# A graph network on one core: the weights' product in four pieces, deviations of x for up to four row tiles at once, a projection's two copies side by side

## The chip, the cores and the metric

The kernel runs on one core of a Trainium2 chip. The metric is the device time of one execution in microseconds (us); the time before is the median of three runs. One more execution was recorded by the hardware profiler; the page, the timelines and the waits below are of that one.

## The reference, cut to what matters

Two layers work on x (3327 rows of 256) and a sparse matrix adj (3327 x 3327). The change lies ahead of the first attention of layer 0; what it touches is the normalised input h, the keys and queries, and the products of h with U1.

```
h = maximum(layernorm(x), 0)            # rows: (x - mean) / sqrt(var + 1e-5)
# layer 0, two steps n; Xf = Xa = h at first
R = (adj + I) / rowsum
q = Xa @ W1.T @ W2.T ;  k = Xa @ W3.T
A = top_p(softmax(q @ k.T), 0.9)        # keep the largest until 0.9, rescale
Xf = R @ Xf ;  Xa = A @ Xa
Z += Xf @ U1[n].T + Xa @ U2[n].T
x = x + layernorm(h + Z)
# layer 1: h = maximum(layernorm(x), 0), attention over neighbours, elu
x = x + elu(attend(h @ W, adj))
```

## The kernel before, in words

Rows are padded to 26 tiles of 128. The work is cut into pieces, each a Python function with an engine, a length in us, a rank and needs. Class Plan (L470) plays these pieces through with the lengths it was given and lists them in the order in which they would start; L564 then issues them in that order. On the chip each engine runs its own list strictly in order and waits on semaphores, so a length is no time on the chip: it only settles the order. "take" and "give" count buffers (two px banks of PSUM, two pl, three kq, four mv, and so on), so that a piece that can't have its buffer is put later.

The start of the kernel goes like this. Function weights (L689) is one piece on PE: it issues the DMAs of W1, W2, W3, U1, U2 on ACT's queue, turns W1 (L703), copies it (L705), multiplies it by W2 (L707) and copies the product into wqk (L709), once for each half of 128 input columns. SP issues the 26 loads of x (L1725). Function prepare (L1108) then makes nine kinds of piece for each row tile t:

- DVE: mean and variance of the tile (measure, L673: L676, L678);
- POOL: 1/sqrt(var + eps) and -mean times that (L681: L683, L684, L686), on one column each;
- ACT: h = relu(x * scale + bias), in place (L1118);
- PE: two transposes of h into a pl bank (L1123); DVE copies them to c (L1126);
- PE: projection by wqk into a px bank (L1131), which gives keys on one half of the partitions and queries on the other;
- ACT: copy to kq (L1137), and of the queries' half straight into qq (L1138);
- POOL: the keys' half from kq to kt (L1141); SP: a DMA of the queries' half to the other half of the partitions of qq (L1144). kq is given back when both are done;
- for even t, sums of keys and their products: a transpose (L745), an ACT copy (L749), a product (L754) and additions to gk on DVE (L766).

Function project_u (L1163) multiplies c of a tile by both steps' U1 into one px bank (L1169), ACT copies one half of the result to main (L1172) and DVE the other half back to c (L1173), after ACT. These 26 products are wanted by the full products (class Full, L1052, with L1074) and can lie anywhere after prepare of their tile.

After the keys of all tiles come statistics of the logits (stats, L770: L781, L786, L792 and on, with a power on POOL at L811), and for each row tile a search (L1368): logits (L856), exponentials on ACT (L870), the row's sum (L879), a guess (POOL L883 to L885, ACT L890 to L893), counts of 3327 columns on ACT (L907) with steps on POOL (L916 on), a window on DVE (L962, L967), and the dropping of what is too small (L1017). Then attention (L1420) turns the row's weights (L1030), ACT copies them (L1035) and PE multiplies (L1042).

```
L1727        weighed = plan.put("PE", 3.0, -200.0, weights, lag=2.0)
L1728        loads = [plan.put("SP", 0.58, -200.0 + t, load_x, t) for t in range(NT)]
L1729        parts = [prepare(t, loads[t]) for t in range(NT)]
L1732        sources = [project_u(t, -1.9 + 0.001 * t) for t in range(NT)]
```

Of the kernel before, what the change touches and what calls it, by code (L numbers as in the profile page):

```python
# [10 lines left out]
F32 = mybir.dt.float32  # L11
# [4 lines left out]
ALU = mybir.AluOpType  # L16
# [3 lines left out]
P = 128  # L20
N = 3327
NT = 26
NP = NT * P
D = 256
DA = 64
# [5 lines left out]
LN_EPS = 1e-5  # L31
# [15 lines left out]
PIECES = 16  # L47
# [5 lines left out]
BUFS = dict(kk=2, e=4, sc=6, f=3, xa=2, xt=2, kq=3, ystage=2, base=1, mv=4, cum=2)  # L53
# [517 lines left out]
def fast(  # L571
# [18 lines left out]
    V, S, T, GP = nc.vector, nc.scalar, nc.tensor, nc.gpsimd  # L590
# [3 lines left out]
    ident = const.tile([P, P], F32, name="ident")  # L594
# [19 lines left out]
    powers = const.tile([P, 4], F32, name="powers")  # L614
# [10 lines left out]
    def half_of(t):  # L625

        r = side(t)
        lo = t // 8 * 512 + (t % 4 * P if t < NT - 1 else 0)
        return slice(r * DA, r * DA + DA), slice((1 - r) * DA, (2 - r) * DA), slice(lo, lo + P)

    with ExitStack() as l0:
        wpool = l0.enter_context(tc.tile_pool(name="wpool", bufs=1))
        small = l0.enter_context(tc.tile_pool(name="small", bufs=2))
# [15 lines left out]
        qq = wpool.tile([P, NT, P], F32, name="qq")  # L649
# [9 lines left out]
        wqk = wpool.tile([P, 2, 2, P], F32, name="wqk")  # L659
# [13 lines left out]
        def measure(src):  # L673

            st = small.tile([P, V.BN_STATS_DIM], F32, name="bst", bufs=3)
            V.bn_stats(st, src)  # L676
            mv = small.tile([P, 4], F32, name="mv", bufs=4)
            V.bn_aggr(mv[:, :2], st)  # L678
            return mv

        def reciprocal_deviation(mv, both=True):  # L681

            GP.tensor_scalar(mv[:, 2:3], mv[:, 1:2], LN_EPS, None, ALU.add)  # L683
            GP.tensor_tensor(mv[:, 2:3], mv[:, 2:3], powers[:, 0:1], ALU.pow)  # L684
            if both:
                GP.tensor_scalar(mv[:, 3:4], mv[:, 0:1], -1.0, mv[:, 2:3], ALU.mult, ALU.mult)  # L686


        def weights():  # L689
            w1 = etpool.tile([P, 4, P], F32, name="et")  # L690
            w1 = w1[:, 0, :].rearrange("p (c o) -> p c o", c=2)
            w2 = small.tile([P, PIECES, 8], F32, name="cands").rearrange("p c r -> p (c r)")[:DA, :DA]
            nc.scalar.dma_start(w1, w1t.rearrange("(c p) o -> p c o", p=P))
# [132 lines left out]
        plan = Plan(dict(rows=1, pl=2, px=2, acca=1, accf=1, accf0=1, accf1=1, et=3, at=4, y=1, e2=3, mask=2, **BUFS))  # L826

        class Row:

# [195 lines left out]
            def turn(self, g):  # L1025
                m = min(4, NT - 4 * g)
                pt = self.pt[g] = ps_x.tile([P, 4, P], F32, name="px")
                for k in range(m):
                    j = 4 * g + k
                    T.transpose(pt[:, k, :], self.e[:, j * P : (j + 1) * P], ident)  # L1030
# [21 lines left out]
        class Full:  # L1052
# [55 lines left out]
        def prepare(t, load):  # L1108
            mine, other, cols = half_of(t)
            held = {}  # L1110
            h = rhs[0][:, t, :]

            def first():
                held["mv"] = measure(h)

            def relu():
                mv = held["mv"]
                S.activation(h, h, AF.Relu, bias=mv[:, 3:4], scale=mv[:, 2:3])  # L1118

            def turn():  # L1120
                held["pt"] = ps_l.tile([P, 2, 512], F32, name="pl")
                for k in range(2):
                    T.transpose(held["pt"][:, 0, k * P : (k + 1) * P], h[:, k * P : (k + 1) * P], ident)  # L1123

            def copy():
                V.tensor_copy(c[:, t, :], held["pt"][:, 0, :D])  # L1126

            def project():
                ps = held["ps"] = ps_x.tile([P, P], F32, name="px")
                for k in range(2):  # L1130
                    T.matmul(  # L1131
                        ps, wqk[:, k, side(t), :], c[:, t, k * P : (k + 1) * P], start=(k == 0), stop=(k == 1)
                    )

            def share():
                held["kq"] = small.tile([P, P], F32, name="kq", bufs=BUFS["kq"])
                S.copy(held["kq"], held["ps"])  # L1137
                S.copy(qq[other, t, :], held["ps"][other])  # L1138

            def keys():  # L1140
                GP.tensor_copy(kt[mine, cols], held["kq"][mine])  # L1141
# [5 lines left out]
            a = plan.put("DVE", 0.62, r, first, needs=[load], take=["mv"])  # L1147
            a = plan.put("POOL", 1.1, r, lambda: reciprocal_deviation(held["mv"]), needs=[a])
            a = hs[0][t] = plan.put("ACT", 0.6, r, relu, needs=[a], give=["mv"])
# [12 lines left out]

        def project_u(t, rank):  # L1163
            held = {}

            def product():
                ps = held["ps"] = ps_x.tile([P, 2 * D], F32, name="px")
                for k in range(2):
                    T.matmul(ps, c[:, t, k * P : (k + 1) * P], u1[:, k, :], start=(k == 0), stop=(k == 1))  # L1169
# [3 lines left out]
            e = plan.put("DVE", 0.43, -2.6, lambda: V.tensor_copy(c[:, t, :], held["ps"][:, D:]), needs=[b], give=["px"])  # L1173
            return b, e

        def finish1(row, done, rank):
# [550 lines left out]
        weighed = plan.put("PE", 3.0, -200.0, weights, lag=2.0)  # L1727
        loads = [plan.put("SP", 0.58, -200.0 + t, load_x, t) for t in range(NT)]  # L1728
        parts = [prepare(t, loads[t]) for t in range(NT)]  # L1729
        keys, sums = [a for a, _ in parts], [b for _, b in parts]  # L1730
        layer1_ready = None
        sources = [project_u(t, -1.9 + 0.001 * t) for t in range(NT)]  # L1732
        right, fresh, failed = None, None, []
        for n in range(STEPS):
# [7 lines left out]
            for k in range(3):  # L1742
                p = stats(cuts[k], cuts[k + 1], base + (-50.0, -2.35, 0.0)[k], [keys, fresh], scaled)
# [102 lines left out]
```

## Time and profile before

| what | value |
|---|---|
| median of 3 runs | 2241.94 us (2241.08 to 2243.65) |
| the profiled execution's own time | 2240.52 us |
| its span, first to last instruction | 2238.6 us |
| PE, DVE, ACT, POOL busy, share of the span | 97%, 72%, 65%, 41% |
| granted TensorE clock, mean | 0.994 |
| PE busy from 0 to 10 us / from 10 to 15 us | 0.88 / 3.71 us |
| key copies of tiles to kt (L1141) | 26, from 15.30 to 55.10 us |
| first statistics product (L781) / first logits (L856) | 58.30 / 59.06 us |
| first transposes of row 0 (L1030) | 111.55 us |

How to read the profile: a group's line gives the source line, the engine, the operation, output <- inputs, shapes and count, then its busy time, the mean length of one in ns, and the idle time of the engine ahead of it with what ended that. A timeline line gives start and length in us, and in brackets how long the engine had been idle and on what. A line of the stage view gives the stretch, its length and each engine's busy time with its number of instructions. A PE product of two operands shows as two records, a transpose as one. ACT's first operation, a table load at 7.91 us, stands behind the DMAs that ACT issues itself.

### The profile page before, as it was taken

The page shows a single profiled execution, that of the slowest core. Times are in us where ns is not written, and L with a number is a line of the kernel's source. Part 1 is how long each engine was busy: PE and PEld are TensorE (multiplying, and loading weights), DVE is VectorE, ACT ScalarE, POOL GpSimd, SP SyncE. Part 2 cuts the span into 40 slices and gives each one's busy share as a digit, 9 for nine tenths or more (in the row PEclk, how much of TensorE's full clock was granted, in tenths as well). Part 3 has the DMA queues.
Part 4 walks back from the last instruction along what each step waited for, and adds up shares of the span by engine and source line. Part 5 has one row for each costly group of instructions (what it writes and reads, how often), then busy time and mean ns, then how long its engine had stood idle before and what let it go on. Part 6 is the DMA issues. An engine that isn't in the chain of part 4 may idle for free.

```text
span 2238.6 us, 36037 instructions
## 1 busy us (share of the span) xinstructions
PE 2177.3 (97%) x11978; PEld 1537.8 (69%) x11978; DVE 1615.0 (72%) x4229; ACT 1455.7 (65%) x2795; POOL 925.1 (41%) x2214
## 2 busy tenths in 40 slices
PE   7999999999999999999999999999999999999997
PEld 5487778777887778877878887887887433333332
DVE  5576657546655744178979877888777998989895
ACT  5776686566566652478887877878774455464653
POOL 6455355435544541256656666566653200000000
PEclk9999999999999999999999999999999999999998
DMA  3012221212212222621212222222225344444341
GB/s 99 20 38 70 68 70 54 70 49 64 70 53 70 70 83 67 191 76 56 76 49 70 59 74 72 81 62 66 69 75 154 121 129 137 116 144 119 102 128 42
DMA packets 192036, 183.76 MB, mean 82 GB/s; under 512 B 15354, under 2 KB 146144, under 8 KB 191712
## 3 DMA queue, kind: packets, MB, share of 16 engines
q1 hardware_dynamic: 189856, 180.10, 27.6%
q8 instruction: 96, 1.57, 0.3%
q10 hardware_dynamic: 1984, 1.26, 0.2%
q14 instruction: 100, 0.82, 0.1%
HBM read 164.41 MB, written 15.94 MB: 81 GB/s over the span
## 4 chain that ended last, share of the span: by engine, by line
PE 75%; ACT 8%; POOL 6%; DVE 5%; issue 3%; DMA 1%; SPq 0%; ACTq 0%; POOLq 0%; DVEq 0%
PE acca L1042 20%; PE accf L1074 20%; PE pl L1608 12%; PE px L1030 6%; PE pl L856 6%; ACT junk L907 5%; PE acca L1622 3%; PE accf L1622 3%; PE px L1217 2%; POOL sc L920 1%; PE px L1312 1%; PE px L1169 1%; DVE cands L967 1%; DVE y L962 1%; ACT et L1035 1%
## 5 line engine op out<-in xcount | busy, mean ns | idle before, releaser
L1042 PE MATMUL acca<-rhs,et 128*128 128x256 f32 x2704 | 619.4, 380 | 1.0 <-ACT et L1035 0.9
L907 ACT ACTIVATE junk<-e,sc 128x3327 fp8e5<-128x3327 f32 x182 | 559.2, 3073 | 48.1 <-POOL sc L952 46.8
L1042 PEld LDWEIGHTS acca<-rhs,et 128*128 128x128 f32 x2704 | 499.9, 191 | 64.4 <-ACT et L1035 2.9
L1074 PE MATMUL accf<-c,at 128*128 128x256 f32 x1352 | 313.5, 382 | 5.5 <-ACT f L1081 5.5
L1074 PE MATMUL accf<-main,at 128*128 128x257 f32 x1352 | 312.0, 382 | 5.6 <-DMA at<-in_adjt_dram 5.3
L962 DVE SCALAR_TENSOR_TENSOR y<-e,sc 128x1664 f32<-128x1664 f32 x104 | 209.0, 2010 | 149.0 <-POOL sc L949 147.0
L1074 PEld LDWEIGHTS accf<-main,at 128*128 128x128 f32 x1352 | 252.8, 191 | 47.9 <-issue 6.5
L1074 PEld LDWEIGHTS accf<-c,at 128*128 128x128 f32 x1352 | 250.0, 190 | 47.7 <-ACT f L1081 10.3
L1035 ACT COPY et<-px 128x512 f32<-128x512 f32 (+1 forms) x364 | 192.7, 553 | 136.1 <-PE acca L1042 72.9
L967 DVE MAX8 cands<-y 128x8 f32<-128x208 f32 x832 | 242.6, 361 | 3.6
L1017 DVE SCALAR_TENSOR_TENSOR e<-e,thr 128x832 f32<-128x832 f32 x208 | 213.1, 1082 | 2.2 <-DVE thr L1012 0.5
L870 ACT ACTIVATE e<-pl 128x1024 f32<-128x1024 f32 x208 | 179.0, 864 | 37.7 <-PE pl L856 37.5
L1581 ACT ACTIVATE et<-at 128x448 bf16<-128x448 f32 (+1 forms) x204 | 112.2, 550 | 137.3 <-DVE e L1592 81.5
L1030 PE MATMUL px<-ident,e 128*128 128x128 f32 x1352 | 191.2, 275 | 9.2 <-DVE gk L766 4.5
L1030 PEld LDWEIGHTS px<-ident,e 128*128 128x128 f32 x1352 | 159.5, 141 | 51.8 <-issue 15.3
L1608 PE MATMUL pl<-e,main 128*64 128x416 f32 x1024 | 187.2, 515 | 0.0
L856 PE MATMUL pl<-kt,qq 64*128 64x512 f32 (+1 forms) x832 | 173.5, 535 | 0.0
L1608 PEld LDWEIGHTS pl<-e,main 128*64 128x64 f32 x1024 | 71.0, 137 | 107.3 <-issue 92.0
L1592 DVE SCALAR_TENSOR_TENSOR e<-c,low,et 128x832 f32<-128x832 f32 x128 | 128.6, 1072 | 8.2 <-PE accf L1622 3.9
L856 PEld LDWEIGHTS pl<-kt,qq 64*128 64x128 f32 x832 | 71.6, 186 | 82.1 <-issue 75.7
L1592 DVE SCALAR_TENSOR_TENSOR e<-qq,low,et 128x832 f32<-128x832 f32 x120 | 120.5, 1074 | 2.6 <-ACT e L1668 2.0
L1580 ACT ACTIVATE at<-at 128x448 f32<-128x448 f32 (+1 forms) x204 | 109.8, 538 | 11.9 <-DMA at<-in_adjt_dram 11.8
(507 smaller groups left out, 2987.3 us busy)
## 6 DMA issues: line engine op xcount, KB each, us to landing
at<-in_adjt_dram SPq DMA_DIRECT2D x414, 256.0 KB
at<-in_adjt_dram SPq DMA_DIRECT2D x102, 192.0 KB
at<-in_adjt_dram SPq DMA_DIRECT2D x52, 128.0 KB
ys<-ystage SPq DMA_DIRECT2D x26, 256.0 KB
rhs<-in_x_dram SPq DMA_DIRECT2D x26, 128.0 KB
ystage<-in_x_dram SPq DMA_DIRECT2D x26, 128.0 KB
base<-ys SPq DMA_DIRECT2D x26, 128.0 KB
x1s<-ystage SPq DMA_DIRECT2D x26, 128.0 KB
```

The lines of the kernel that those rows point to most:

```text
L856: T.matmul(pl[:, r, :m], qq[half, self.i, :], kt[half, 512 * k : 512 * k + m], start=True, stop=True,)
L870: S.activation(self.e[:, 1024 * k : 1024 * k + 2 * w].rearrange("p (r w) -> p r w", r=2), pl, AF.Exp, accum_out=(self.p0, self.p1, self.p2 ...
L907: S.activation(junk[:, :N], self.e[:, :N], fn, bias=t, scale=-1.0, accum_out=dst, saturate=False)
L962: V.scalar_tensor_tensor(self.y[:, : hi - lo], self.e[:, lo:hi], self.up, self.e[:, lo:hi], ALU.is_lt, ALU.mult, accum_out=(self.h0, self. ...
L967: V.max(self.cands[:, o // PIECE, :], self.y[:, o - lo : min(o + PIECE, hi) - lo])
L1017: V.scalar_tensor_tensor(piece, piece, self.thr[:, o : o + 1], piece, ALU.is_gt, ALU.mult)
L1030: T.transpose(pt[:, k, :], self.e[:, j * P : (j + 1) * P], ident)
L1035: S.copy(self.et[g][:, :m, :], self.pt.pop(g)[:, :m, :])
L1042: T.matmul(self.acc, et[:, j - 4 * g, :], rhs[self.n][:, j, :], start=(j == 0), stop=(j == NT - 1))
L1074: T.matmul(self.acc[:, : self.w], self.at[j // JC][:, j % JC, :], self.src[:, j, : self.w], start=(j == 0), stop=(j == NT - 1),)
L1592: V.scalar_tensor_tensor(held["e"][:, k, :], extra["both"][b % 2][:, k, :], low[:, j, k : k + 1], held["mask"], ALU.max, ALU.mult,)
L1608: T.matmul(q["acc"][a][k * FH : (k + 1) * FH, c, :C], main[:, j, h * FH : (h + 1) * FH], held["e"][:, h, c * C : (c + 1) * C], start=(j == 0),
```

## The change

Four edits in the first stage.

- weights becomes four pieces: both halves of W1 are turned into one px bank, copied to two tiles ("rest" and a kq), multiplied into one px bank, and copied to wqk with two copies for both halves at once. They have needs and buffers of their own, and the first is planned to come 8 us after the start. The DMAs are issued ahead of the plan, on the same queue and in the same order.
- Mean and variance go to columns of one tile mvs for a group of one to four row tiles (the groups begin at 0, 1, 2, 4, 6, 8, 11, 14, 18, 22; three buffers). POOL then does four instructions a group, on as many columns as it has tiles, in place of three a tile: -mean times the factor is now a product and a multiplication by -1. A group's buffer is given back after its last relu.
- The queries' half is copied to qq by POOL from kq, after the keys, and no longer by ACT from PSUM. The piece on ACT is given 0.3 in place of 0.55 us, that on POOL 0.7 in place of 0.35.
- In project_u DVE's copy needs the product and no longer ACT's copy; the bank is given back when both are done.

The diff, cut to its core:

```diff
             nc.scalar.dma_start(w1, w1t.rearrange("(c p) o -> p c o", p=P))
...
-            for k in range(2):
-                ps = ps_x.tile([DA, P], F32, name="px")
-                T.transpose(ps, w1[:, k, :], ident)
-                w1r = small.tile([P, P], F32, name="kq", bufs=BUFS["kq"])[:DA]
-                S.copy(w1r, ps)
-                ps = ps_x.tile([P, DA], F32, name="px")
-                T.matmul(ps, w1r, w2, start=True, stop=True)
+            def turn():
+                held["ps"] = ps_x.tile([DA, 2, P], F32, name="px")
+                for k in range(2):
+                    T.transpose(held["ps"][:, k, :], w1[:, k, :], ident)
+            def copy():
+                for k in range(2):
+                    S.copy(w1r[k], held["ps"][:, k, :])
+            def product():
+                held["ps"] = ps_x.tile([P, 2, DA], F32, name="px")
+                for k in range(2):
+                    T.matmul(held["ps"][:, k, :], w1r[k], w2, start=True, stop=True)
+            def place():
                 for r in range(2):
-                    S.copy(wqk[:, k, r, (1 - r) * DA : (2 - r) * DA], ps)
+                    S.copy(wqk[:, :, r, (1 - r) * DA : (2 - r) * DA], held["ps"])
+            a = plan.put("PE", 0.25, -200.0, turn, take=["px"], needs=[plan.put("SP", 0.02, -201.0, lambda: None, lag=8.0)])
+            a = plan.put("ACT", 0.5, -200.0, copy, needs=[a], take=["kq"], give=["px"])
+            a = plan.put("PE", 0.25, -200.0, product, needs=[a], take=["px"], give=["kq"])
+            return plan.put("ACT", 0.5, -200.0, place, needs=[a], give=["px"])
...
+        def deviations(lo, hi):
+            m, held = hi - lo, {}
+            def first(k):
+                if k == 0:
+                    held["mv"] = small.tile([P, 4, 4], F32, name="mvs", bufs=3)
+                st = small.tile([P, V.BN_STATS_DIM], F32, name="bst", bufs=3)
+                V.bn_stats(st, rhs[0][:, lo + k, :])
+                V.bn_aggr(held["mv"][:, k, :2], st)
+            def rest():
+                mv = held["mv"][:, :m]
+                GP.tensor_scalar(mv[:, :, 2], mv[:, :, 1], LN_EPS, None, ALU.add)
+                GP.tensor_tensor(mv[:, :, 2], mv[:, :, 2], powers[:, 0:1].to_broadcast([P, m]), ALU.pow)
+                GP.tensor_tensor(mv[:, :, 3], mv[:, :, 0], mv[:, :, 2], ALU.mult)
+                GP.tensor_scalar(mv[:, :, 3], mv[:, :, 3], -1.0, None, ALU.mult)
...
+            a = plan.put("POOL", 1.1 + 0.2 * m, -100.0 + lo, rest, needs=[a])
...
             def share():
                 held["kq"] = small.tile([P, P], F32, name="kq", bufs=BUFS["kq"])
                 S.copy(held["kq"], held["ps"])
-                S.copy(qq[other, t, :], held["ps"][other])
             def keys():
                 GP.tensor_copy(kt[mine, cols], held["kq"][mine])
+                GP.tensor_copy(qq[other, t, :], held["kq"][other])
...
-            a = plan.put("ACT", 0.55, r, share, needs=[a], take=["kq"], give=["px"])
-            k = plan.put("POOL", 0.35, r, keys, needs=[a])
+            a = plan.put("ACT", 0.3, r, share, needs=[a], take=["kq"], give=["px"])
+            k = plan.put("POOL", 0.7, r, keys, needs=[a])
...
-            e = plan.put("DVE", 0.43, -2.6, lambda: V.tensor_copy(c[:, t, :], held["ps"][:, D:]), needs=[b], give=["px"])
+            e = plan.put("DVE", 0.43, -2.6, lambda: V.tensor_copy(c[:, t, :], held["ps"][:, D:]), needs=[a])
+            plan.put("SP", 0.0, -2.6, lambda: None, needs=[b, e], give=["px"], lag=0.0)
...
+        GROUPED = (0, 1, 2, 4, 6, 8, 11, 14, 18, 22, NT)
```

More of the change, by code (lines that the diff above doesn't have):

```diff
@@ L689, in weights @@
         def weights():
+            held = {}
             w1 = etpool.tile([P, 4, P], F32, name="et")
@@ L692, in weights @@
             w2 = small.tile([P, PIECES, 8], F32, name="cands").rearrange("p c r -> p (c r)")[:DA, :DA]
+            w1r = small.tile([P, PIECES * 8], F32, name="rest", bufs=1)[:DA].rearrange("p (k o) -> p k o", k=1)
+            w1r = [w1r[:, 0, :], small.tile([P, P], F32, name="kq", bufs=BUFS["kq"])[:DA]]
             nc.scalar.dma_start(w1, w1t.rearrange("(c p) o -> p c o", p=P))
@@ L824, in stats @@
             return plan.put("DVE", 0.6, rank, rest, needs=[a])
-        plan = Plan(dict(rows=1, pl=2, px=2, acca=1, accf=1, accf0=1, accf1=1, et=3, at=4, y=1, e2=3, mask=2, **BUFS))
+        plan = Plan(dict(rows=1, mvs=3, pl=2, px=2, acca=1, accf=1, accf0=1, accf1=1, et=3, at=4, y=1, e2=3, mask=2, **BUFS))
         class Row:
@@ L1106, in keys_summed, with prepare @@
             return plan.put("DVE", 0.4, rank, gather, needs=[a], give=[tags[1], "kk"])
-        def prepare(t, load):
+        def deviations(lo, hi):
[12 more added lines that the diff above has]
+                GP.tensor_scalar(mv[:, :, 3], mv[:, :, 3], -1.0, None, ALU.mult)
+            a = []
+            for k in range(m):
+                a.append(
+                    plan.put("DVE", 0.62, -100.0 + lo + k, first, k, needs=[loads[lo + k], a], take=["mvs"] * (k == 0))
+                )
+            a = plan.put("POOL", 1.1 + 0.2 * m, -100.0 + lo, rest, needs=[a])
+            return {lo + k: (a, held, k, k == m - 1) for k in range(m)}
+        def prepare(t, measured):
             mine, other, cols = half_of(t)
+            ready_, mvs, k_, last = measured
             held = {}
             h = rhs[0][:, t, :]
-            def first():
-                held["mv"] = measure(h)
             def relu():
-                mv = held["mv"]
+                mv = mvs["mv"][:, k_, :]
                 S.activation(h, h, AF.Relu, bias=mv[:, 3:4], scale=mv[:, 2:3])
@@ L1146, in prepare @@
             r = -100.0 + t
-            a = plan.put("DVE", 0.62, r, first, needs=[load], take=["mv"])
-            a = plan.put("POOL", 1.1, r, lambda: reciprocal_deviation(held["mv"]), needs=[a])
-            a = hs[0][t] = plan.put("ACT", 0.6, r, relu, needs=[a], give=["mv"])
+            a = hs[0][t] = plan.put("ACT", 0.6, r, relu, needs=[ready_], give=["mvs"] * last)
             a = plan.put("PE", 0.25, r, turn, needs=[a], take=["pl"])
@@ L1722, in fast @@
         LAST = NT - 4
+        GROUPED = (0, 1, 2, 4, 6, 8, 11, 14, 18, 22, NT)
         def load_x(t):
             nc.sync.dma_start(rhs[0][:, t, :], x[t * P : (t + 1) * P, :])
-        weighed = plan.put("PE", 3.0, -200.0, weights, lag=2.0)
+        weighed = weights()
         loads = [plan.put("SP", 0.58, -200.0 + t, load_x, t) for t in range(NT)]
-        parts = [prepare(t, loads[t]) for t in range(NT)]
+        measured = {}
+        for lo, hi in zip(GROUPED, GROUPED[1:]):
+            measured.update(deviations(lo, hi))
+        parts = [prepare(t, measured[t]) for t in range(NT)]
         keys, sums = [a for a, _ in parts], [b for _, b in parts]
```

## The prediction

> **What bounds the kernel now.** I read the page first: TensorE (PE) is busy 97% of the span, so only an edit that takes waits out of PE can shorten the run. Then I read busy time by stage, to see where PE waits inside the part that the change touches.
>
> ```profile
> PE 2177.3 (97%) x11978; PEld 1537.8 (69%) x11978; DVE 1615.0 (72%) x4229; ACT 1455.7 (65%) x2795; POOL 925.1 (41%) x2214
> ```
> ```profile
> core 0: us, PE busy (x) PEld busy (x) DVE busy (x) ACT busy (x) POOL busy (x), PEclk, DMA share, GB/s
> ...
> 20.00:25.00 5.00, 4.76 (x31) 3.47 (x30) 3.98 (x16) 3.98 (x12) 4.11 (x13) 1.00 0.06 13
> 25.00:30.00 5.00, 3.26 (x24) 2.63 (x24) 4.37 (x16) 3.18 (x12) 3.99 (x13) 1.00 0.12 26
> 30.00:35.00 5.00, 4.69 (x34) 3.74 (x32) 3.47 (x13) 3.74 (x13) 4.07 (x13) 1.00 0.12 27
> ```
> The stage runs until 58.30 us, when the first statistics product (L781) follows the last projection. In it GpSimd (POOL) has about 4 us of work in every 5, and what is left of each 5 us is its gaps of 0.03 to 0.1 us between dependent instructions: it is the bound. Its groups in the first 80 us, and the same power operation at other widths:
> ```profile
> L684 POOL TENSOR_TENSOR mv<-mv,powers 128x1 f32<-128x1 f32 x26 | 14.8, 567 | 2.2
> ...
> L1141 POOL COPY kt<-kq 64x128 f32<-64x128 f32 x26 | 7.4, 287 | 6.7 <-ACT kq L1137 6.0
> L686 POOL TENSOR_SCALAR mv<-mv 128x1 f32<-128x1 f32 x26 | 6.9, 265 | 2.8
> ...
> L683 POOL TENSOR_SCALAR mv<-mv 128x1 f32<-128x1 f32 x26 | 5.8, 222 | 6.8 <-DVE mv L678 4.9
> ...
> L811 POOL TENSOR_TENSOR sig<-stat,powers 128x10 f32<-128x10 f32 x1 | 2.0, 1969 | 0.9 <-DVE stat L807 0.9
> ...
> L811 POOL TENSOR_TENSOR sig<-stat,powers 128x3 f32<-128x3 f32 x1 | 0.9, 869 | 5.9 <-DVE stat L807 5.9
> ```
> A tile's three deviation instructions start 0.30, 0.68 and 0.35 apart and its key copy takes 0.33: 1.66 us a tile, 24.41 to 26.09 and again to 27.77 on the timeline. Last I read PE's timeline from there to the first transposes of row 0 (L1030):
> ```profile
> 72.47 7.40 PE L1169 MATMUL px<-late,c 128*128 128x512 f32 x16 [1.85 <-DVE c L1173]
> ...
> 92.49 3.70 PE L1169 MATMUL px<-late,c 128*128 128x512 f32 x8 [0.53 <-DVE c L1173]
> 97.53 5.60 PE L1169 MATMUL px<-late,c 128*128 128x512 f32 x12 [1.34 <-DVE c L1173]
> ...
> 109.73 1.98 PE L1169 MATMUL px<-late,c 128*128 128x512 f32 x4 [1.57 <-DVE c L1173]
> 111.55 0.60 PE L1030 MATMUL px<-ident,e 128*128 128x128 f32 x4
> ```
> L1169 is project_u, four records and 1.76 us a tile (81.19 to 89.97 holds five). It fills PE while row 0 is searched: 7 tiles lie before 58.30, 19 after. PE waits 5.3 us in it, each time for a px bank that ACT and then DVE must empty; ACT is in a 3.07 us count (L907) meanwhile. After 123.84, where it waits 0.53, PE hardly waits up to 200 us.
>
> [...] 567 ns for 1 column, 869 for 3, 1969 for 10, so 0.15 us a column. [...] Seen here at L883, 0.31 us alone and 2.04 beside the DVE window at 88.91; the 26 key copies all took 0.29[...]. [...] whichever of project_u's two copies comes first, the other still waits for its semaphore. [...]
>
> **The change, part by part.** Times are of the profiled execution (2240.52 = span 2238.6 + 1.9); the median of the runs is 1.4 above it, so a gain is taken off either alike. I follow the built order of the changed kernel with the durations above.
>
> *Start.* ACT's first operation stays behind its DMA issues and the table load (7.91 to 9.19). Before, the weights came next and relu 0 at 11.84; now relus 0 to 3 go first, from 9.2, the w1 copies lie behind them, and the last copy to wqk behind relu 5. Relu 5 needs the group of tiles 4 and 5, whose mvs buffer is freed by relu 0 (9.8); behind c of tile 0, aggregation is done at 11.6, POOL's 1.72 us at 13.4, relu 5 at 14.5. First projection: about 15.1 instead of 13.71. So the weights' four pieces lose 1.4 us at their own spot. What hides it is the next limit: the fourth key waits for a kq buffer whose DMA (L1144) is queued on SP behind the 26 loads of x, first issued at 17.07.
>
> *Deviations.* A group of m costs four instructions: 0.30 + (0.68 + 0.15(m-1)) + 0.29 + 0.30 = 1.57 + 0.15(m-1). The fourth and the wide forms aren't in the trace; below, the narrow row (1.57 whatever m), above, every one 0.15 a column (2.9 for m = 4); I take the formula, since only the power is dear. Ten groups: 15.7 + 16 x 0.15 = 18.1 us, against 26 x 1.33 = 34.6.
>
> *Copies.* qq leaves ACT (26 x 0.26) and goes to POOL as a second 64x128 copy: 26 x 0.33 = 8.6 us. POOL in all: 34.6 + 8.6 = 43.2 before, 18.1 + 17.2 = 35.3 after. In the built order: six groups, keys 0 to 7, a group, keys 8 to 10, three groups of four (2.03 each), keys 11 to 25. With POOL's starts as above, keys 7 end near 24.9, keys 10 near 28.8, the groups near 34.9.
>
> *Tail.* ACT has relus 18 to 21 ahead of key copy 11, which so comes at 35.0. From then kq's three buffers set the pace: copy, DMA issue, landing, next copy. Before, the tightest such cycle is 34.85 to 37.38 on ACT's timeline, with L1138 inside it:
> ```profile
> 34.85 0.27 ACT L1137 COPY kq<-px 128x128 f32<-128x128 f32 x1
> 35.15 0.26 ACT L1138 COPY qq<-px 64x128 f32<-64x128 f32 x1
> ...
> 37.38 0.27 ACT L1137 COPY kq<-px 128x128 f32<-128x128 f32 x1 [0.48 <-POOL kt L1141]
> ```
> 2.53 less 0.27 is 2.26 for three tiles, 0.75 a tile; POOL's 0.66 fits under it. Tiles 12 and 13 follow within 1.2 us (relu 22 lies between); four cycles later, 9.0 us, come 24 and 25, at 45.0 to 45.2. Two tiles of project_u stand ahead of the first logits: 45.2 + 0.1 + 2 x 1.76 + 0.2 for the products between them = **49.0**, where before it was 58.30. Gain **9.3**. (If a cycle took no less than the 2.53, it would be 50.1.)
>
> *Given back.* Only 4 tiles of project_u lie ahead of that now, so 22 come after it: 3 x 1.76 = **5.3** of PE work moved behind.
>
> *Side by side.* DVE no longer stands behind ACT by plan, but the bank still serialises them. Where DVE goes first, during a count, the bank is free when ACT's copy ends, 0.42 us sooner. Walking the 22 tiles against ACT's queue, PE waits 1.1 and 0.5 after row 0's two counts, 0.2 and 1.75 after row 1's, then 1.7 when row 0's second group of transposes needs the bank of tile 26, whose ACT copy stands behind row 2's first count: 5.2, against 5.3 + 0.5 before. Gain **0.6**. The loads of adjt for full row 0 are issued right behind the last key DMA in both, so these products don't wait.
>
> Sum: 9.3 - 5.3 + 0.6 = 4.6 us. From about row 340 of PE's 2976 rows on, both built orders are the same, so with PE the bound the shift should last to the end; what follows later waits for PE's own results and moves with it. **2241.94 - 4.6 = 2237.3.** A measurement can tell about 0.2%, 4.5 us, from no change: this stands just beyond it.
>
> **Rivals.** *The gain is paid back in PE waits* (no change). ACT gains 22 tiles to empty between counts instead of 19. If each added tile meets a count as the worst one did (1.85), less the 0.42, waits rise by 3 x 1.43 = 4.3 rather than fall by 0.6: 9.3 - 5.3 - 4.3 = -0.3. Half of that gives 9.3 - 5.3 - 2.2 = 1.8, so 2240.1. For it: ACT has 22 us of queued work in a row around the first transposes. Against: rows 1 and 2 are searched some 10 us earlier, which relieves ACT later. A late tail acts alike: first logits at 52 instead of 49.0 leave 1.6.
>
> *POOL is blocked* (slower). It would be the 52 key copies in the tail: a copy of c us costs 15 x (2c - 0.75) + 11 x (2c - 0.66) there. At 0.33 nothing; at c = 0.44 it costs 15 x 0.13 + 11 x 0.22 = 4.4 and the gain is about gone; from 0.53 it costs 9.1 and the kernel is slower by 0.2%. At 0.55: 5.25 + 4.84 = 10.1, so 2247.4. Against: 26 of 26 copies at 0.29 with DVE active beside them.
>
> **Numbers.** Faster 0.50 (2237.3), no change 0.42 (2240.1), slower 0.08 (2247.4). Low end: the key pace is POOL's 0.66 (15 x 0.09 = 1.4), half of the waits fall away (2.6) and the later groups cost half of their extra columns (0.8): 2237.3 - 4.8 = 2232.5. High end: half of the added waits and the late tail at once, 9.3 - 3.0 - 5.3 - 2.2 = -1.2: 2243.0. About 0.1 is left out on either side.
>
> **What would show it.** In the profile after: relu 0 near 9.2 and first projection near 15.1; four wide instructions a group, 1.0 us for the power at four columns; the last kq copy near 45; first logits (they now stand ahead of the statistics product) near 49; PE's waits between there and the first transposes about 3.5. The forecast is wrong if key copies 11 to 25 take over 0.85 us a tile, if logits start after 51, or if waits on px exceed 7.

## The result, and the profile after

The changed kernel takes 2237.05 us (median of 12 runs, 2234.35 to 2238.71) against 2241.27 of the kernel before beside it (12 runs): 4.2 us less, ratio 0.9982 with a 95% interval of 0.9974 to 0.9991. The forecast was 2237.3. The interval excludes no change, but reaches to both sides of the 0.2%. The profiled execution of the changed kernel is the slowest of its 12 (2238.71, span 2236.6), so the two profiled executions lie only 1.8 us apart. The median of a second measurement, below, is 6.4 us under the kernel before.

The first line of the page after, and the stage view for the same stretch as before:

```profile
PE 2176.2 (97%) x11978; PEld 1538.7 (69%) x11978; DVE 1614.4 (72%) x4229; ACT 1449.1 (65%) x2767; POOL 922.1 (41%) x2202
```
```profile
core 0: us, PE busy (x) PEld busy (x) DVE busy (x) ACT busy (x) POOL busy (x), PEclk, DMA share, GB/s
20.00:25.00 5.00, 4.88 (x38) 4.23 (x37) 3.95 (x17) 3.20 (x11) 2.93 (x11) 1.00 0.12 28
25.00:30.00 5.00, 4.26 (x25) 2.93 (x25) 3.80 (x17) 2.99 (x9) 4.24 (x14) 1.00 0.17 38
30.00:35.00 5.00, 4.18 (x23) 2.45 (x22) 4.75 (x18) 3.57 (x8) 4.26 (x10) 1.00 0.00 0
```

PE has 13.3 us of work in these 15 us where it had 12.7. POOL has 11.4 in place of 12.2: it has room from 20 to 25 and is as full as before from 25 to 35, where the groups of four lie. POOL's groups in the first 80 us:

```profile
L1183 POOL COPY qq<-kq 64x128 f32<-64x128 f32 x26 | 7.5, 290 | 1.2
L1182 POOL COPY kt<-kq 64x128 f32<-64x128 f32 x26 | 7.5, 289 | 3.9 <-ACT kq L1179 3.0
L1140 POOL TENSOR_TENSOR mvs<-mvs,powers 128x4 f32<-128x4 f32 x3 | 3.1, 1040 | 0.2
L1140 POOL TENSOR_TENSOR mvs<-mvs,powers 128x2 f32<-128x2 f32 x3 | 2.1, 714 | 0.3
...
L1140 POOL TENSOR_TENSOR mvs<-mvs,powers 128x3 f32<-128x3 f32 x2 | 1.8, 888 | 0.2
...
L1140 POOL TENSOR_TENSOR mvs<-mvs,powers 128x1 f32<-128x1 f32 x2 | 1.1, 572 | 0.2
```

The power takes 0.57, 0.71, 0.89 and 1.04 us at one to four columns: 0.14 to 0.17 a further column. All 52 copies take 0.29. The stage ends at 49.34, where the first logits (L873) start; before, it ended at 58.30, with the first statistics product. PE's timeline before,

```profile
58.30 0.83 PE L781 MATMUL px<-gk,qq 128*128 128x129 f32 x6
```

and after, from there to the first transposes (L1047):

```profile
49.34 1.99 PE L873 MATMUL pl<-kt,qq 64*128 64x512 f32 x8
...
63.21 10.83 PE L1209 MATMUL px<-late,c 128*128 128x512 f32 x24 [1.48 <-ACT main L1212]
...
89.45 1.98 PE L1209 MATMUL px<-late,c 128*128 128x512 f32 x4 [1.21 <-DVE c L1213]
92.32 3.70 PE L1209 MATMUL px<-late,c 128*128 128x512 f32 x8 [0.88 <-ACT main L1212]
...
108.15 0.60 PE L1047 MATMUL px<-ident,e 128*128 128x128 f32 x4
110.31 1.14 PE L1047 MATMUL px<-ident,e 128*128 128x128 f32 x8 [1.56 <-ACT main L1212]
```

Its waits for px sum to 3.6 up to the first transposes, and 1.56 more ahead of the second group of them. Where both kernels have done the same work, at the second logits of row 3, the changed kernel stands at 128.78 and the one before at 131.74, with 1.83 us of products (L1074) still to come that the other has behind it: a lead of 4.8 us.

### The profile page after: what moved, and what is told of

Same layout as the page of the kernel before. It is cut to its first block, busy times and chain, and to the rows that moved or that the text cites. A ratio compares the mean times of both kernels' runs of the same rounds, so it can differ in the third digit from the quotient of the medians.

```text
span 2236.6 us, 35974 instructions
## 1 busy us (share of the span) xinstructions
PE 2176.2 (97%) x11978; PEld 1538.7 (69%) x11978; DVE 1614.4 (72%) x4229; ACT 1449.1 (65%) x2767; POOL 922.1 (41%) x2202
## 4 chain that ended last, share of the span: by engine, by line
PE 77%; ACT 9%; DVE 5%; POOL 4%; issue 3%; DMA 2%; SPq 0%; ACTq 0%; DVEq 0%; POOLq 0%
PE acca L1059 20%; PE accf L1091 20%; PE pl L1649 12%; PE pl L873 6%; PE px L1047 6%; ACT junk L924 5%; PE acca L1663 3%; PE accf L1663 3%; PE px L1258 2%; PE px L1209 1%; PE px L1353 1%; POOL sc L937 1%; DMA at<-in_adjt_dram 1%; ACT et L1052 1%; DVE e L1633 1%
## 5 line engine op out<-in xcount | busy, mean ns | idle before, releaser
L1047 PE MATMUL px<-ident,e 128*128 128x128 f32 x1352 | 191.6, 275 | 7.3 <-ACT et L1052 2.3
L1047 PEld LDWEIGHTS px<-ident,e 128*128 128x128 f32 x1352 | 160.2, 141 | 47.4 <-issue 12.1
L873 PE MATMUL pl<-kt,qq 64*128 64x512 f32 (+1 forms) x832 | 173.5, 535 | 0.0
L873 PEld LDWEIGHTS pl<-kt,qq 64*128 64x128 f32 x832 | 71.6, 186 | 83.9 <-issue 77.9
```

Source lines behind the costliest of these rows:

```text
L873: T.matmul(pl[:, r, :m], qq[half, self.i, :], kt[half, 512 * k : 512 * k + m], start=True, stop=True,)
```

## The experiments

"First products" below are the first logits or the first statistics product, whichever comes first; "ahead" counts the tiles of project_u that lie before them. PE idle is the span less PE's busy time, both of the profiled execution. Executions of one kernel scatter by 4 to 9 us, so a difference of 1 us between two medians is not told.

| kernel | median, us (runs) | ratio to before, 95% | first products | ahead | PE idle |
|---|---|---|---|---|---|
| before | 2241.3 to 2241.6 | 1 | 58.30 | 7 | 61.3 |
| changed | 2237.05 (12) | 0.9982, 0.9974 to 0.9991 | 49.34 | 4 | 60.4 |
| changed, again | 2235.20 (8) | 0.9974, 0.9964 to 0.9985 | 47.63 | 4 | 59.2 |
| three narrow instructions a tile | 2246.79 (7) | 1.0027, 1.0015 to 1.0038 | 58.88 | 4 | 64.7 |
| queries' copy on ACT | 2236.85 (9) | 0.9977, 0.9967 to 0.9987 | 48.91 | 4 | 58.3 |
| the same to tile 10 | 2236.77 (11) | 0.9980, 0.9971 to 0.9989 | 49.45 | 4 | 58.6 |
| weights in one piece | 2242.75 (13) | 1.0006, 0.9998 to 1.0015 | 51.75 | 3 | 63.5 |
| the same, no early filler | 2240.28 (21) | 0.9996, 0.9989 to 1.0002 | 53.57 | 4 | 59.8 |
| DVE's copy behind ACT's | 2244.30 (21) | 1.0013, 1.0006 to 1.0020 | 48.48 | 4 | 63.5 |
| PE busy from 2 us | 2236.22 (19) | 0.9981, 0.9974 to 0.9988 | 49.62 | 4 | 53.5 |
| loads of U later | 2233.14 (5) | 0.9960, 0.9947 to 0.9974 | 45.41 | 4 | 56.6 |
| three fillers ahead | 2232.98 (6) | 0.9964, 0.9952 to 0.9976 | 52.98 | 7 | 55.9 |
| both of these | 2232.59 (5) | 0.9958, 0.9945 to 0.9972 | 50.74 | 7 | 53.1 |
| U later, ten ahead | 2233.54 (5) | 0.9964, 0.9950 to 0.9978 | 55.74 | 10 | 55.3 |

(In the row "PE busy from 2 us", PE's added products are no idle time.) The two measurements of the changed kernel together have a median of 2236.45 over 20 runs; differences below are from that.

The theory at the start: POOL's work ahead of key 11 sets the first logits, from there on PE is the bound, and a shift lasts. The rivals: the copies' move earns the gain; the gain is lost late; the pieces of the weights are free or cost something.

### The changed kernel again

> The changed kernel once more, for what one profile differs from the next. In the profile shown the lead over the kernel before is 4.8 us at the third row's second logits (128.78), 4.2 at 799 us and 2.9 after the wait for adjt at 804 to 810, where PE stands 6.6 us against 5.3 before; 2.0 at the end. Theory (what is lost late is how that DMA fell in one execution): the time is 4 to 5 us under the kernel before, first logits again near 49.3, and the wait for adjt somewhere else between 5 and 7. Rival (the lead is lost for a reason, each time): the wait for adjt is 6.6 again within 0.2, and the lead at the end no more than 2.5.

Measured: 6.4 us under the kernel before, more than the 4 to 5 of the theory, first logits at 47.63 and not near 49.3, the wait for adjt at 5.8 (6.6 in the first profile). The rival, 6.6 again, fell: the late loss at that place varies from one execution to the next. The first logits vary too, by 1.7 us, and this has a cause that the forecast had not seen. First the changed kernel, then the same kernel again, on PE's timeline:

```profile
17.24 1.06 PE L1165 MATMUL pl<-ident,rhs 128*128 128x128 f32 x4
18.09 0.42 PE L762 MATMUL acca<-ident,kq 128*128 128x128 f32 x1
```
```profile
17.09 0.64 PE L1165 MATMUL pl<-ident,rhs 128*128 128x128 f32 x4
17.56 0.27 PE L762 MATMUL acca<-ident,kq 128*128 128x128 f32 x1
```

The same instructions take 1.06 in one and 0.64 in the other, and 0.42 against 0.27. PE works at about half its later rate from its first product on (1.18 for the first four transposes in both profiles, 0.64 at 17.09 in the second); the switch comes near 20.2 in one execution and 17.1 in the other. At half rate 3.1 us more cost about 1.5 of the 1.7, an estimate: half of the 3.1. The moment differs from one execution to the next, between 16 and 20.5 us in these profiles, and so does the time from PE's first product to it: 10 us in one execution and 7 in the other, though not without gaps. What sets the moment is not shown.

### Deviations: three narrow instructions for each tile

```diff
-                GP.tensor_scalar(mv[:, :, 2], mv[:, :, 1], LN_EPS, None, ALU.add)
-                GP.tensor_tensor(mv[:, :, 2], mv[:, :, 2], powers[:, 0:1].to_broadcast([P, m]), ALU.pow)
-                GP.tensor_tensor(mv[:, :, 3], mv[:, :, 0], mv[:, :, 2], ALU.mult)
-                GP.tensor_scalar(mv[:, :, 3], mv[:, :, 3], -1.0, None, ALU.mult)
+                for k in range(m):
+                    reciprocal_deviation(mv[:, k, :])
```

> All as changed, in the same order on each engine, but a group's deviations are again three POOL instructions for each tile. Theory (POOL's work ahead of key 11 is what sets the first logits): 1.33 us a tile in place of 1.57 + 0.15(m-1) a group; following POOL's order, groups (4,5) from 12.1, keys 0 to 7 to 26.8, keys 8 to 10 to 32.9, last group to 48.8 where it was 35.5: first logits 49.3 + 13.3 = 62.6 and, with PE waiting for all of it, 2250 (2247 to 2253), slower than the kernel before. Rival (POOL's share is hidden by the key buffers' DMA cycle): at most 4 us over the changed kernel, 2237 to 2241.

Measured: 2246.79, first logits at 58.88. POOL's last group ends at 46.9 in place of 35.5. ACT's timeline shows who waits for whom, a relu a tile and each one behind POOL:

```profile
35.04 0.60 ACT L1160 ACTIVATE rhs<-rhs,mvs 128x256 f32<-128x256 f32 x1 [0.72 <-POOL mvs L686]
36.36 0.60 ACT L1160 ACTIVATE rhs<-rhs,mvs 128x256 f32<-128x256 f32 x1 [0.72 <-POOL mvs L686]
37.68 0.60 ACT L1160 ACTIVATE rhs<-rhs,mvs 128x256 f32<-128x256 f32 x1 [0.72 <-POOL mvs L686]
```

They start 1.32 apart, POOL's time for a tile. The first logits come 10.4 later than the 48.5 that the changed kernel has on average in its two profiles, and the time is 10.3 longer: one to one. The theory's mechanism holds, its numbers were too high: 62.6 and 2250 (2247 to 2253) against 58.88 and 2246.79. POOL's last group ended at 46.9 and not at 48.8, and the tail behind it was shorter by the other 1.8, as ACT copies keys 11 to 13 while POOL still has the last groups. The rival, at most 4 us, falls. PE's granted clock is at 0.50 from about 36.7 to 47.0 us in this kernel (two transposes take 0.44 at 35.69 and 0.69 at 37.01), in a stretch with little work for PE and no wait above 1.64; the first logits wait for POOL there in any case.

### Queries' copy back on ACT, for all tiles and for tiles 0 to 10

```diff
                 S.copy(held["kq"], held["ps"])
+                S.copy(qq[other, t, :], held["ps"][other])
...
                 GP.tensor_copy(kt[mine, cols], held["kq"][mine])
-                GP.tensor_copy(qq[other, t, :], held["kq"][other])
```

> All as changed, in the same order, but ACT copies the queries' half of every tile from PSUM to qq, as before, and POOL copies the keys alone. Theory (POOL is the bound up to key 11, ACT has room there, and in the tail the key buffers and PE set the pace): POOL has 11 x 0.34 = 3.7 us less ahead of key 11, of which PE's own work leaves about 1.5 (it waits 0.74 + 0.57 + 0.17 between 26 and 34 us); the tail's pace goes from 0.72 to 0.75 a tile, 0.5 lost: first logits 48.3, time 1 us under the changed kernel. Rival (moving the copy from ACT is part of what earns the gain, ACT being short in the tail): first logits at 51 or later, 2239 or more.

> As the run before, but ACT copies the queries' half only for tiles 0 to 10, and POOL for tiles 11 to 25. Theory: POOL's 3.7 us less ahead of key 11 without the slower tail: first logits about 47.8, 1.5 us under the changed kernel. Rival (ACT is short in the tail): clearly faster than the run before, by 2 us or more. Rival (POOL isn't the bound ahead of key 11): no different from the changed kernel, first logits 49.3 within 0.3.

Measured: 2236.85 and 2236.77, first logits at 48.91 and 49.45, all as in the changed kernel. POOL's 3.7 us less ahead of key 11 buys nothing. Of the first of the two kernels, ACT's timeline and then POOL's:

```profile
30.31 0.37 ACT L1212 COPY main<-px 128x256 f32<-128x256 f32 x1 [1.52 <-PE px L1209]
30.57 4.04 ACT L1160 ACTIVATE rhs<-rhs,mvs 128x256 f32<-128x256 f32 x8
```
```profile
30.57 0.25 POOL L1142 TENSOR_SCALAR mvs<-mvs 128x4 f32<-128x4 f32 x1
32.03 0.23 POOL L1139 TENSOR_SCALAR mvs<-mvs 128x4 f32<-128x4 f32 x1 [1.21 <-DVE mvs L1135]
```

POOL has the group of tiles 14 to 17 done at 28.76, but relu 14 stands in ACT's queue behind the copy of a filler, which waits 1.52 for PE. Then eight relus in a row lead up to key 11, and POOL itself waits 1.21 for DVE. In the changed kernel the same group ends at 31.42 and relu 14 starts at 31.70, behind that same copy: POOL and ACT's queue are level there. So more work on POOL shows in full, less of it does not: the 1 to 1.5 us of the theory did not come, and for less work the rival holds that POOL isn't the bound ahead of key 11. The two rivals on ACT being short fall.

### The weights in one piece

The four pieces are one function on PE again, as in the kernel before; the planner lays out the rest.

> All as changed, but the weights' product is one piece of PE again, as before, and the planner lays the rest out anew around it. First projection again at 13.7, where the changed kernel has it at 15.4. Prediction's step (the 1.7 us are hidden, since POOL and the key buffers are what comes next): the time is that of the changed kernel within 0.8 us. Rival (PE starts its dense work later with the pieces, and its first products, at half the later rate until 17 to 20 us, are on the path): faster than the changed kernel by 1 to 2 us. Rival (the pieces earn part of the gain, since relus 0 to 3 no longer stand behind the weights): slower by 1 us or more.

Measured: 2242.75, 6.3 us slower than the changed kernel, no gain over the kernel before left. That the pieces gain nothing, as the prediction had it, fell; the rival, that they earn part of the gain, held. Two causes stood open, and the next kernel parts them.

```diff
-            a = plan.put("PE", 1.75, rank, product, needs=[turned_h[t], weighed], take=["px"])
+            a = plan.put("PE", 1.75, rank, product, needs=[turned_h[max(t, 10)], weighed], take=["px"])
```

> As the kernel with the weights in one piece (2242.75), but no tile of project_u may run before tile 10 has been turned. There, a filler of 3.52 us at half rate stood between the first and the second projection, and relus 0 and 1, late behind the weights' copies, held back POOL's second group of two until 14.06, where the changed kernel has it at 12.1. Theory A (the filler is what costs): second key near 16 in place of 19.2, and 3 to 5 us of the 6 come back, 2238 to 2240. Theory B (the buffers of the deviations, which wait for relus 0 and 1, are what costs): no more than 1.5 us comes back, 2241 or more.

Measured: 2240.28, between the two theories. The second key comes at 17.48 in place of 19.17. But the first logits come at 53.57 with four tiles ahead, against 51.75 with three: a tile is 1.76, so for equal work this is no earlier. In the first stage the filler cost nothing. What did is seen in ACT's and POOL's timelines of this kernel,

```profile
12.12 1.10 ACT L1160 ACTIVATE rhs<-rhs,mvs 128x256 f32<-128x256 f32 x2
```
```profile
14.65 0.23 POOL L1139 TENSOR_SCALAR mvs<-mvs 128x2 f32<-128x2 f32 x1 [6.25 <-DVE mvs L1135]
```

beside those of the changed kernel:

```profile
9.59 2.08 ACT L1160 ACTIVATE rhs<-rhs,mvs 128x256 f32<-128x256 f32 x4
```
```profile
12.10 0.23 POOL L1139 TENSOR_SCALAR mvs<-mvs 128x2 f32<-128x2 f32 x1 [3.52 <-DVE mvs L1135]
```

With the weights' six copies to kq and wqk ahead of relu 0 on ACT, it comes 2.5 later. The mvs buffer that it gives back comes 2.5 later, and with it POOL's second group of two. At the end of the stage this is 4.2 us against the first profile (53.57 against 49.34) and 5.9 against the second, and the time is 3.8 us longer. So the pieces bring the relus forward, and with them the groups; this is shown for 2.5 us. The rest of the stage's loss is not traced to the pieces: the planner laid out the rest anew. The first of these two kernels is 2.5 us slower still. On its PE timeline stands a long wait in the search:

```profile
116.49 0.66 PE L1047 MATMUL px<-ident,e 128*128 128x128 f32 x4 [3.13 <-ACT main L1212]
```

The granted clock is at 0.50 from about 117.1 to 120.5 behind that wait. The two are large enough for the 2.5 us, but no run parts them from the rest.

### DVE's copy of project_u behind ACT's

```diff
-            e = plan.put("DVE", 0.43, -2.6, lambda: V.tensor_copy(c[:, t, :], held["ps"][:, D:]), needs=[a])
-            plan.put("SP", 0.0, -2.6, lambda: None, needs=[b, e], give=["px"], lag=0.0)
+            e = plan.put("DVE", 0.43, -2.6, lambda: V.tensor_copy(c[:, t, :], held["ps"][:, D:]), needs=[b], give=["px"])
```

> All as changed, but in project_u the DVE copy again needs ACT's copy and gives the bank back; the planner lays the rest out anew. Prediction's step (where DVE goes first during a count, the bank is free 0.42 us sooner): 0.6 us slower than the changed kernel, PE's waits for px between first logits and first transposes near 4.2 in place of 3.6. Rival (the bank serialises the copies either way, and the layout decides): within 0.5 us of the changed kernel or faster.

Measured: 2244.30, 7.9 us slower than the changed kernel and slower than the one before. Up to 49 us it goes as the changed kernel does. In project_u PE waits 5.3 for px again, in the same four amounts as before the change, within 0.01, and 0.25 at the transposes; in the changed kernel these are 3.6 and 1.56. That is the predicted step: 0.4 in place of 0.6. The rest lies behind it, on PE's timeline and in the stage view:

```profile
114.01 1.14 PE L1047 MATMUL px<-ident,e 128*128 128x128 f32 x8 [2.83 <-ACT et L1052]
```
```profile
112.00:114.00 2.00, 0.00 (x0) 0.00 (x0) 1.97 (x7) 2.00 (x4) 0.73 (x2) 1.00 0.00 0
114.00:116.00 2.00, 1.99 (x12) 1.72 (x13) 1.89 (x8) 2.00 (x2) 0.00 (x0) 0.82 0.00 0
116.00:118.00 2.00, 2.00 (x6) 1.64 (x5) 1.73 (x12) 1.98 (x3) 0.29 (x2) 0.50 0.00 0
118.00:120.00 2.00, 2.00 (x9) 1.67 (x9) 1.75 (x11) 1.56 (x6) 0.58 (x3) 0.82 0.00 0
```

The number behind the five engines is the granted clock. PE waits 2.83 for ACT's copy of the transposed weights, which stands in ACT's queue between counts; then the clock is at 0.50 for (1.00 - 0.82) x 2 / 0.5 + 2 + (1.00 - 0.82) x 2 / 0.5 = 3.4 us, which costs 1.7 by an estimate, half of that. At 145.72 it happens again, after 3.09. Against the second profile of the changed kernel PE is idle 4.3 us longer (63.5 less 59.2) and busy 4.5 longer (2178.9 less 2174.4), of which twice 1.7 are these. In this profile the first half rate ends at 19.73 us, in that one at 17.16, which is about 1.3 more. It is shown that this layout costs 8 us, and where. The rival's number, within 0.5 us or faster, fell; that the layout decides did not. Whether the edit in itself brings more than the 0.4 isn't: the planner set the counts and the copies elsewhere as well, and a kernel with this order and the old copies was not tried.

### Work for PE from the start

```diff
+            ps = ps_x.tile([P, 2, P], F32, name="px")
+            [T.transpose(ps[:, k % 2, :], ident, ident) for k in range(40)]
```

> All as changed, in the same order, but PE begins with 40 transposes of the identity into a px bank, from about 2 us until about 9, whose output nobody reads. In the four profiles of this order a product takes twice its later time until a moment between 17.1 and 20.3 us, which differs from one execution to the next. Theory ([...] the start of the changed kernel has PE on the path): transposes of tile 0 take 0.60 for four in place of 1.18, first logits near 46.8, the executions scatter less, time 1.5 to 2 us under the changed kernel. Rival (the slow products are hidden behind POOL and ACT): first logits no earlier than 47.6, time the same.

Measured: 2236.22, no change. The transposes end at 7.77, and PE then waits 2.53 for relu 0. The stage view:

```profile
10.00:12.00 2.00, 1.44 (x8) 0.80 (x8) 1.37 (x5) 2.00 (x6) 0.09 (x1) 0.90 1.06 358
12.00:14.00 2.00, 1.20 (x5) 0.90 (x6) 1.73 (x8) 0.46 (x2) 1.59 (x6) 0.50 0.90 266
14.00:16.00 2.00, 2.00 (x11) 1.88 (x11) 1.83 (x7) 1.72 (x6) 1.05 (x3) 0.50 0.81 255
16.00:18.00 2.00, 2.00 (x11) 2.00 (x11) 1.30 (x6) 0.88 (x3) 1.13 (x2) 0.50 0.88 246
```

When relu 0 comes the products have their later times (two transposes of W1 take 0.38 at 11.06, and 0.64 in the changed kernel), and the clock falls to 0.50 from about 11.6 to 18.4. So this run doesn't tell what a full rate there is worth, neither for the theory nor for its rival: the rate was not held. In the other profiles this column shows 1.00 in these stretches, though the products take the same times as here: 1.06 for four transposes at 17.24 in the changed kernel, 1.06 at 17.04 here. So in those profiles the half rate at the start is read from the products' times and not from the column.

### Loads of U later, three fillers ahead, and both

First edit: ACT no longer issues the four DMAs of U1 and U2; SP issues them in double(t), behind the queries' DMAs of tiles 0, 1, 24 and 25. Second edit:

```diff
-        sources = [project_u(t, -1.9 + 0.001 * t) for t in range(NT)]
+        sources = [project_u(t, -60.0 if t < 7 else -1.9 + 0.001 * t) for t in range(NT)]
```

> All as changed, in the same order, but the four DMAs of U1 and U2 are no longer issued by ACT ahead of its first operation: SP issues U1's behind the first two DMAs of queries, and U2's behind the last two. ACT's table load then starts near 3 us in place of 8.3, and relu 0 waits only for POOL, near 5.4 in place of 9.6. Theory (the start is bound by ACT's queue, and each us that the keys come earlier lasts to the end, PE being busy from there on): first logits 2 to 3 us earlier than the 47.6 to 49.4 seen, 46 or so; time 2 us under the changed kernel. Rival (the loads of x and POOL set the pace from tile 4 on): first logits within 0.7 of 48.5, time the same.

> All as changed, but seven tiles of project_u are ranked ahead of the logits, so that three more of them (5.3 us of PE) lie ahead of the first logits, as before the change, and 19 after. Theory (PE's work is only moved, and what counts is PE's waits): first logits near 54, 5.3 us later, and the time that of the changed kernel within 1 us. Rival (the first logits start the search, and the search sets the end): 4 to 5 us slower than the changed kernel, no better than the kernel before.

> The two variants that were faster at once: U's loads behind the keys' DMAs on SP, and seven tiles of project_u ahead of the logits. Theory (one takes waits out of PE's start, 3.3 us, the other out of its search of the first rows, 3.5 us, and both last): 2229 to 2231. Rival (both take away the same late waits, those for adjt): 2232 to 2233.

> As the run before, with ten tiles of project_u ahead of the logits. Theory (each filler in the search may meet a count on ACT and wait for its bank, while one ahead of it doesn't): 0.5 to 1 us less than the run before. Rival (PE runs out of fillers in the search, and the first transposes wait for the counts): 2 us more than the run before, with PE idle between 80 and 110 us.

Measured: 2233.14, 2232.98, 2232.59 and 2233.54. Each is some 3.5 us under the changed kernel, together they give no more, and their intervals overlap. With U later, ACT's timeline starts so:

```profile
3.46 1.28 ACT L1160 ACT_TABLE_LOAD   x1 [3.46 <-DVE bst L1134]
5.21 0.60 ACT L1160 ACTIVATE rhs<-rhs,mvs 128x256 f32<-128x256 f32 x1 [0.47 <-POOL mvs L1142]
```

relu 0 comes 4.4 us earlier and the first logits 3.1 (45.41 against 48.5), and the time falls by 3.3, where the theory had 2; the rival, no change, fell. Two things moved with this edit. ACT's queue is free sooner, and SP is done with the loads of x sooner too: the first DMA of queries comes at 14.12 in place of 17.01. Which of the two brings the gain wasn't tested. With three fillers put back, the first products come 4.5 us later, and the time is 3.5 shorter. PE's timeline of that kernel at the transposes:

```profile
104.36 0.60 PE L1047 MATMUL px<-ident,e 128*128 128x128 f32 x4
104.89 1.99 PE L873 MATMUL pl<-kt,qq 64*128 64x512 f32 x8
106.81 1.09 PE L1047 MATMUL px<-ident,e 128*128 128x128 f32 x8
```

The wait of 1.56 ahead of the second group is gone: logits stand there now. Up to 900 us PE waits 15.5 + 8.8 us (0 to 130, 130 to 900) in place of 17.3 + 10.1 in the second profile of the changed kernel; the later part is a wait for adjt at about 220 us that the changed kernel has (1.3 to 1.8) and this one has not. So it is PE's waits that count and not when the first logits start; the rival, 4 to 5 us slower, falls, and the theory's "within 1 us" as well. Both edits together: 2229 to 2231 was expected, and the rival's 2232 to 2233 came, but not for its reason, since PE idle falls by 2.8 us more (53.1 against 55.9). In its place PE is busy 2.6 longer (2177.9 against 2175.3). It starts at 6.0 and works at half rate until 16.5, for 10.5 us in place of 8.3 (9.8 to 18.1 with the fillers alone), which is about 1.1. And its clock falls once more, late, behind a wait of 2.02:

```profile
1708.81 12.31 PE L1091 MATMUL accf<-c,at 128*128 128x256 f32 x48 [2.02 <-ACT f L1098]
```
```profile
1705.00:1710.00 5.00, 2.98 (x13) 2.24 (x12) 3.79 (x5) 3.66 (x8) 0.73 (x1) 0.95 0.48 145
1710.00:1715.00 5.00, 5.00 (x18) 4.16 (x17) 4.83 (x16) 0.00 (x0) 0.73 (x2) 0.71 0.29 72
```

At 0.50, the value in the 2 us stretches further up, that is (0.05 + 0.29) x 5 / 0.5 = 3.4 us, and 1.7 us of time, both estimates. U later alone has the same behind a wait of 1.88; with the fillers alone (1.83) and with ten ahead (1.78) the clock stays at 1.00 there. The fourth version, with ten tiles ahead, gains nothing more: 0.95 slower is neither what the theory nor what the rival said. Each of these four stands on 5 or 6 runs.

## Why the prediction was right, and where its steps were not

- **Start.** Predicted relu 0 at 9.2 and first projection at 15.1: 9.59 and 15.53, both late by ACT's table load, which came 0.4 later in this execution. The prediction counted the pieces as a delay that is hidden, and as no gain. The first holds for the sum; the second is wrong. Without them 3.8 to 6.3 us are lost, of which 2.5 are traced to the groups' buffers, which hang on relus 0 and 1. The order that the prediction followed had this in it, so its times came out right; its reading of the part did not.
- **Deviations.** Predicted 2.03 for a group of four: 2.05 to 2.08. Keys 7, keys 10 and the groups were to end near 24.9, 28.8 and 34.9: 25.55, 29.33 and 35.52, late by the start's 0.4 and some 0.2. That POOL's groups are on the path is shown by the narrow instructions: each us by which the first logits came later was one us of time.
- **Copies.** 52 at 0.29: POOL is not blocked, that rival is refuted. In the search one POOL instruction (L900) took 2.04 at 80.89, beside the DVE window, 0.32 at 56.84 and 0.30 at 101.35; why the copies beside DVE kept their 0.29 is not shown. As an edit by itself it is worth nothing that could be measured, in either direction.
- **Tail.** Predicted 35.0 for key 11 and 45.0 to 45.2 for the last two: 35.65, 45.10 and 45.78. (45.78 - 35.65) / 14 = 0.72 a tile against 0.66 to 0.75. In the second profile it is (44.07 - 33.94) / 14 = 0.72 again; with the queries on ACT (45.16 - 34.52) / 14 = 0.76. First logits: 49.0 against 49.34 and 47.63. The near hit on the first is in part luck, since the scatter, 1.7 us between the two profiles with PE's slow first products in it, was not in the forecast.
- **Given back.** 5.3 us of products did move behind. The sum is right, but it had a better place for them: three of them ahead of the logits are 3.5 us faster.
- **Side by side.** Predicted waits of 1.6, 1.95 and 1.7, 5.2 in all: 1.48, 1.21 + 0.88 and 1.56 came, 5.1. Where DVE goes behind ACT again, these are 5.5, so the step of 0.6 is 0.4. That the two copies of a bank go one behind the other came as predicted: in the profile after, DVE's copies wait 7.0 us for ACT's, in six places, and ACT's 1.3 for DVE's, in three. What it left out is the layout: the one that the planner makes without this edit costs 7.9, in part by waits of 3 us for ACT's copies and the clock behind them.
- **The shift lasts.** Its lead of 4.8 at 129 us is 4.2 at 799. In between PE waits 1.75 at 221 us for adjt, which it now reaches before the DMA, and no longer waits 2.4 for gk (4.5 less 2.1). What the two profiles lose behind 799 us is the wait for adjt at 804 (6.6 against 5.3) and 0.9 in small pieces; in the second profile it is 5.8. The rival in which the waits eat the gain did not come.

What the forecast said of an edit alone (the pieces hidden, 0.6 for the copies side by side) is not what undoing it costs. The forecast held because it followed the built order as a whole: 4.6 us less were forecast, 4.2 came in the first measurement and about 5 in both together. (The sum for the high end of the range comes to 2243.1, not 2243.0.)

## What to carry to other kernels

Where a planner lays out the order, sum the built order and not the edits: undoing one edit of four here cost 0, 4 to 6, 8 or 10 us, 22 to 24 in all, for a change that brings 5. Before moving filler work, look at which wait it stands behind: put it where no engine's long instruction holds its buffer. In these counts the planner's new layout of everything else is included. And count the clock with a long wait of PE: waits of 2.83, 3.09 and 3.13 us were each followed by 0.50 for 3.4 us here, by an estimate 1.7 more of time.

## What was not expected of the hardware

- After PE had stood for 2.83 us its granted clock was at 0.50 for 3.4 us; waits up to 1.6 us at the same place left it at 1.00. Elsewhere it fell behind waits of 1.88 and 2.02 and stayed at 1.00 behind one of 1.83, and with narrow instructions it was at 0.50 for 10 us in a stretch of little work, with no wait above 1.64. So these runs show no one length of wait at which it falls.
- PE's first products take twice their later time (1.18 and 0.60 us for four 128x128 transposes) until a moment between 16 and 20.5 us.
- The power on POOL takes 0.57 us for one column and 0.14 to 0.17 for each further one, four columns 1.04.
- ACT's issue of the last two loads of U was held (they start at 6.31 and 7.77, the one before at 3.71, each taking 0.4 to 0.5), and its table load with it; without these four DMAs the table load starts at 3.46 in place of 8.29.
